# A graph layer on one Trainium2 core: each group's sums leave as 124 rows instead of 128

## The chip, the core and the metric

The program runs on one core of one Trainium2 chip. The metric is the device time of one execution in microseconds, and lower is better. Three executions of the kernel before took 2150.35, 2143.92 and 2141.62 us; the median is 2143.92 us.

## The reference, cut to what matters

There are 6250 nodes of 256 features and 100000 edges. Each edge has a source, a destination and two attributes, and the edges come **sorted by destination**. A graph attention layer comes first, then an expert layer; both add to `x`.

```python
h_fwd = h @ W_forward.T                      # h = layernorm(x); 64 outputs
h_rev = h @ W_reverse.T
messages = h_fwd[src] * direction[:, 0:1] + h_rev[src] * direction[:, 1:2]
scores = leaky_relu(einsum('ef,hf->eh', messages, attn), 0.2)     # 4 heads
exp_scores = exp(scores - scores.max(axis=0))
sum_exp = segment_sum(exp_scores, dst)       # per destination node and head
norm = exp_scores / (sum_exp[dst] + 1e-10)
outs = [segment_sum(messages * norm[:, hd:hd+1], dst) for hd in range(4)]
x = x + concat(outs)                         # 4 x 64 = 256 features
...
x = x + expert_layer(layernorm(x))           # 8 experts, the best one per token
```

So each node needs 260 sums over its incoming edges: 4 heads times 64 weighted message values, and 4 sums of exponentials. The change touches how these 260 sums per node reach memory.

## The kernel before

The kernel is one function, `tile_gnn_ffn_kernel`. A second function, `general_path`, computes the same for any input and runs at the end only if a flag says that the input broke an assumption of the first.

**Node table.** The first part (lines 667 to 698) normalises the nodes, multiplies them with the weights and stores `node_tab`, 136 floats (544 bytes) per node.

**Edge stage.** The edges are cut into 782 tiles of 128. Six tiles make a group (`GT = 6`, 131 groups), and two groups make a batch (66 batches). For each batch of 12 tiles, the loop from line 828 does this:

- GpSimd issues 12 indirect DMAs, one per tile (line 833), each gathering 128 rows of 544 bytes from `node_tab` into a slice of `gt`. `gt` has four buffers, so the gathers may run up to four batches ahead.
- VectorE scales and adds the two halves (lines 839 to 848), forms the scores (851 to 859), ScalarE takes the exponential (863), VectorE builds the weighted messages `v` (864, 865) and a matrix `hot` (870) that says which destination, counted from the group's first one, each edge has.
- For each of the two groups, TensorE adds up six products of `hot` and `v` into one PSUM tile `pv` (line 876): row k of it holds the 260 sums of the k-th destination after the group's first. One more small product (line 885) adds what the group before had gathered for the destination that both share.
- ScalarE copies `pv` to `r` in SBUF (line 887, four buffers), and SyncE loads the group's first destination from `base_i` into a register (888) and stores `r` at that row of `sums` (890).

The groups' stores **overlap**. A store always writes 128 rows from the group's first destination on, though the group reaches only as far as the next group's first destination; the store of the next group writes the rest over. So each store has to wait until the one before has landed, and the order of the stores is the order of the groups. Rows that a later store writes over don't matter.

The instruction order on each engine is the program's, reordered by a scheduler when the program is built. ScalarE's queue holds the exponentials and the copies of line 887 in one order, and a copy that waits holds up the exponential behind it. SyncE's queue in this stage holds the register load and the store of each group in turn, and nothing else.

**The check on the input.** `high` (line 759) is, for each group, how many rows further the next group begins. Line 785 sets a flag if any `high` is over 127, since rows between two stores would then be written by none.

**After the edge stage.** ScalarE's queue loads `sums` back in seven pieces `part` (line 951); VectorE divides, adds to `x` and normalises; the tokens are routed (line 1021), the experts run on TensorE (1046 to 1086), and the results are gathered and stored (1091 to 1107).

Of the kernel before, what the change touches and what calls it, by code (L numbers as in the profile page):

```python
# [11 lines left out]
OP = mybir.AluOpType  # L12
AX = mybir.AxisListType

P = 128
# [504 lines left out]
def kernel(  # L520
# [25 lines left out]
    nc = tc.nc  # L546
# [21 lines left out]
    NG = -(-ET // GT)  # L568
    EB = -(-ET // P)
    CHAIN = 16  # L570
    SPREAD = 40.0
    TROWS = N + P - 1
    NSLOT = E * CAP
# [5 lines left out]
    sums = dram.tile([TROWS, ACC], F32, name="sums")  # L579
# [183 lines left out]
    last_tile = local[:, GT - 1:GF * GT:GT]  # L763
    nc.vector.tensor_tensor(carry_from[:, CHAIN:GF], last_tile[:, CHAIN:GF], high[:, CHAIN:GF], OP.is_equal)

# [7 lines left out]
    wrong = ep.tile([P, 5], F32, name="wrong")  # L773
# [8 lines left out]
    nc.vector.tensor_reduce(wrong[:, 1:2], t0, AX.X, OP.max)  # L782
    nc.vector.tensor_scalar(wrong[:, 1:2], wrong[:, 1:2], 0.0, None, op0=OP.is_gt)
    nc.vector.tensor_reduce(wrong[:, 2:3], high, AX.X, OP.max)
    nc.vector.tensor_scalar(wrong[:, 2:3], wrong[:, 2:3], float(P - 1), None, op0=OP.is_gt)
    nc.vector.tensor_reduce(wrong[:, 3:4], high, AX.X, OP.min)
    nc.vector.tensor_scalar(wrong[:, 3:4], wrong[:, 3:4], 0.0, None, op0=OP.is_lt)
    nc.vector.memset(wrong[:, 4:5], 1.0)
    nc.vector.tensor_sub(t0[0:1, CHAIN:GF], high[0:1, CHAIN:GF], last_tile[0:1, CHAIN:GF])
    nc.vector.tensor_reduce(wrong[0:1, 4:5], t0[0:1, CHAIN:GF], AX.X, OP.min)  # L790
    nc.vector.tensor_scalar(wrong[:, 4:5], wrong[:, 4:5], 0.0, None, op0=OP.is_le)
# [19 lines left out]
    with tc.tile_pool(name="p2", bufs=3) as p2, \  # L811
# [8 lines left out]
        def over_partitions(to, t):  # L820

            pm = ps2.tile([P, H, P], F32, name="pm", tag="pv")
            for hd in range(H):
                nc.tensor.transpose(pm[:, hd, :], t[:, hd:hd + 1].to_broadcast([P, P]), ident)
            nc.vector.tensor_reduce(to, pm, AX.X, OP.max)

        before = None
        for b, gs in enumerate(batches):
            i0, i1 = gs[0] * GT, min((gs[-1] + 1) * GT, ET)
            n = i1 - i0  # L830
            gt = p2.tile([P, GB, ROW], F32, name="gt", bufs=4)
            for i in range(i0, i1):
                nc.gpsimd.indirect_dma_start(  # L833
                    out=gt[:, i - i0, :], out_offset=None, in_=node_tab,
                    in_offset=bass.IndirectOffsetOnAxis(ap=srci[:, i:i + 1], axis=0))
            m = p2.tile([P, GB, MS], F32, name="m")

            fac = turns[:, b % 2, 0:2, :]
            nc.vector.tensor_copy(fac[:, :, :n], ea[:, :, i0:i1])
            fw = gt[:, :n, 0:MS]  # L840
            nc.vector.tensor_mul(fw, fw, fac[:, 0, :n].unsqueeze(2).to_broadcast([P, n, MS]))  # L841
            for g in gs:
                a0, a1 = g * GT - i0, min((g + 1) * GT, ET) - i0
                k = a1 - a0
                rv = ps2.tile([P, GT, MS], F32, name="rv", bufs=1)
                nc.vector.tensor_mul(rv[:, :k, :], gt[:, a0:a1, MS:ROW],  # L846
                                     fac[:, 1, a0:a1].unsqueeze(2).to_broadcast([P, k, MS]))
                nc.vector.tensor_add(m[:, a0:a1, :], fw[:, a0:a1, :], rv[:, :k, :])  # L848
            sc = p2.tile([P, GB, H], F32, name="sc")
            s = sc[:, :n, :]  # L850
            nc.vector.scalar_tensor_tensor(s, m[:, :n, O:MS], 0.2, m[:, :n, O:MS],  # L851
                                           op0=OP.mult, op1=OP.max)
            if i1 == ET:
                nc.vector.tensor_scalar(sc[:, n - 1, :], sc[:, n - 1, :], no_edge, None, op0=OP.add)
            nc.vector.tensor_reduce(gmax[:, b, :], s.rearrange("p j h -> p h j"), AX.X, OP.max)
            if b == 0:
                over_partitions(shift, gmax[:, 0, :])
                nc.vector.tensor_copy(shift_p, shift)
            nc.vector.tensor_sub(s, s, shift_p.unsqueeze(1).to_broadcast([P, n, H]))
            v = p2.tile([P, GB, ACC], F32, name="v")  # L860
            w = fixed[:, P + H + (b % 2 * (2 + H) + 2) * GB:P + H + (b % 2 + 1) * (2 + H) * GB]
            w = w.rearrange("p (j h) -> p j h", h=H)
            nc.scalar.activation(v[:, :n, H * O:ACC], s, AF.Exp)  # L863
            nc.vector.tensor_copy(w[:, :n, :], v[:, :n, H * O:ACC])  # L864
            nc.vector.tensor_mul(  # L865
                v[:, :n, 0:H * O].rearrange("p n (h o) -> p n h o", h=H),
                m[:, :n, 0:O].unsqueeze(2).to_broadcast([P, n, H, O]),
                w[:, :n, :].unsqueeze(3).to_broadcast([P, n, H, O]))
            hot = p2.tile([P, GB, P], F32, name="hot")
            nc.vector.tensor_tensor(hot[:, :n, :], lane_p.unsqueeze(1).to_broadcast([P, n, P]),  # L870
                                    local[:, i0:i1].unsqueeze(2).to_broadcast([P, n, P]), OP.is_equal)
            for g in gs:
                tiles = list(range(g * GT, min((g + 1) * GT, ET)))
                pv = ps2.tile([P, ACC], F32, name="pv")
                for i in tiles:
                    nc.tensor.matmul(pv, hot[:, i - i0, :], v[:, i - i0, :], start=(i == tiles[0]),  # L876
                                     stop=(i == tiles[-1] and before is None))
                if before is not None:
                    k = (g - 1) % ZN
                    z = zt[(g - 1) // ZN % 2]  # L880
                    if k == 0:
                        nz = min(ZN, NG - g)

                        nc.vector.tensor_copy(z[:, 0:nz, 0], carry_from[:, g - 1:g - 1 + nz])
                    nc.tensor.matmul(pv, z[:, k, :], before, start=False, stop=True)  # L885
                r = p2.tile([P, ACC], F32, name="r", bufs=4)
                nc.scalar.copy(r, pv)  # L887
                row = nc.values_load(base_i[0:1, g:g + 1], engines=(mybir.EngineType.SP,), min_val=0,
                                     max_val=N - 1, skip_runtime_bounds_check_because="clamped to 0..N-1")
                nc.sync.dma_start(sums[bass.ds(row, P), :], r)  # L890
                before = r if g < CHAIN else v[:, tiles[-1] - i0, :]


# [5 lines left out]
        tiny = const.tile([P, H], F32, name="tiny")  # L899
        nc.vector.tensor_scalar(tiny, over, SPREAD, None, op0=OP.min)  # L900
        nc.scalar.activation(tiny, tiny, AF.Exp)
# [3 lines left out]

        nc.vector.tensor_scalar(bad[:, 0:1], bad[:, 0:1], SPREAD, 0.0, op0=OP.is_le, op1=OP.is_equal)
        nc.vector.tensor_reduce(bad[:, 1:2], wrong, AX.X, OP.max)
# [36 lines left out]
    with tc.tile_pool(name="p4", bufs=2) as p4, \  # L944
            tc.tile_pool(name="ps4", bufs=2, space=bass.MemoryType.PSUM) as ps4:
        for c in range(NCK):
# [48 lines left out]
            for n in range(CH):  # L995
# [12 lines left out]
                                           op0=OP.is_le, op1=OP.mult)  # L1008
# [7 lines left out]
                                    op0=OP.max, op1=OP.min)  # L1016
# [15 lines left out]
    with tc.tile_pool(name="p5", bufs=2) as p5, \  # L1032
# [13 lines left out]
        for e in range(E):  # L1046
# [26 lines left out]
            for a, b in rows:  # L1073
                k = b - a
                py = ps5.tile([P, D], F32, name="py")
                for f in range(FC):
# [8 lines left out]
                                               op0=OP.min, op1=OP.add)  # L1085
# [57 lines left out]
```

## Time and profile before

| what | value |
|---|---|
| median of three runs | 2143.92 us (2141.62 to 2150.35) |
| the profiled execution | 2147.85 us, of it 2146.1 us from the first to the last instruction |
| TensorE clock granted, mean | 0.735 of full speed |
| TensorE matmuls busy | 1146.4 us (53%) |
| VectorE busy | 917.6 us (43%) |
| GpSimd busy | 863.3 us (40%) |
| ScalarE busy | 224.8 us (10%) |
| edge stage, first gather to last store | about 100 to 1412 us |
| experts on TensorE | about 1580 to 2043 us |

All of the profile is of one execution, the one that took 2147.85 us. Busy shares are averages over very different stages, so the stages are read one by one. A row of the timeline gives the start, the duration, the engine, the line, the operation with the tile that it writes and those that it reads, and, in brackets, how long the engine was idle before and what ended that. In the rows, PE is TensorE, PEld its weight load, DVE VectorE, ACT ScalarE, POOL GpSimd, and SPq the queue of SyncE. "issue" means that the profile shows nothing that the engine waited for. A row of a table of stretches gives, for each engine, busy time and, in brackets, the number of instructions.

### The profile page before, as it was taken

To read this page: it belongs to the slowest core of one execution; us is meant where nothing else is said; L and a number is where in the kernel's file an instruction comes from. 1 tells how busy PE (TensorE), PEld (TensorE's weight loads), DVE (VectorE), ACT (ScalarE), POOL (GpSimd) and SP (SyncE) were. 2 spreads that over 40 slices of the span, in tenths; PEclk is the share of its full clock that TensorE was granted. 3 is DMA by queue.
4 is the path that set the end of the run, shared out by engine and by line. 5 is a ranking of instruction groups with operands and counts; after the bars stand their busy time and mean duration, and the time that the engine had idled before them with its cause. 6 is when DMAs were issued, how large, how long until landed. Compare 5 with 4: busy or idle time off the path is not lost. (4 is left out here: it accounts for less than half of the span.)

```text
span 2146.1 us, 13763 instructions
## 1 busy us (share of the span) xinstructions
PE 1146.4 (53%) x4158; PEld 840.2 (39%) x4158; DVE 917.6 (43%) x1827; ACT 224.8 (10%) x506; POOL 863.3 (40%) x896
## 2 busy tenths in 40 slices
PE   6421446434443454444334444545559999999900
PEld 5310334323232333333223333435436666666600
DVE  7540555544444455644345355657612222221134
ACT  2100000000000000000000000012211111111122
POOL 0176655555555665655556665103410000000065
PEclk9755677766666667766666766765569999999955
DMA  8522222222222222222222222162222222211034
GB/s 262 190 58 52 57 55 55 59 54 53 52 57 58 57 57 54 67 59 53 53 56 57 62 58 55 33 202 74 74 82 77 77 77 77 72 57 43 17 107 138
DMA packets 114150, 158.65 MB, mean 74 GB/s; under 512 B 19762, under 2 KB 94289, under 8 KB 113939
## 3 DMA queue, kind: packets, MB, share of 16 engines
q0 software_dynamic: 29728, 67.35, 13.8%
q1 hardware_dynamic: 66734, 74.20, 10.5%
q10 hardware_dynamic: 17604, 16.13, 2.4%
q8 instruction: 35, 0.57, 0.1%
q14 instruction: 49, 0.39, 0.1%
HBM read 107.80 MB, written 49.80 MB: 73 GB/s over the span
## 5 line engine op out<-in xcount | busy, mean ns | idle before, releaser
L833 POOL DMA_INDIRECT gt<-node_tab,srci x782 | 740.0, 946 | 623.0 <-DVE sc L851 278.7
L876 PE MATMUL pv<-v,hot 128*128 128x260 f32 x1564 | 498.1, 477 | 544.9 <-DVE hot L870 381.2
L876 PEld LDWEIGHTS pv<-v,hot 128*128 128x128 f32 x1564 | 370.3, 241 | 656.2 <-issue 578.5
L864 DVE COPY fixed<-v 128x48 f32<-128x48 f32 x66 | 13.9, 210 | 600.8 <-ACT v L863 393.7
L1097 POOL DMA_INDIRECT yg<-ybuf,to_get x49 | 64.9, 1325 | 484.4 <-issue 477.2
L1077 PE MATMUL py<-w2t,hf 128*128 128x256 f32 (+1 forms) x1024 | 222.3, 379 | 0.0
L865 DVE TENSOR_TENSOR v<-m,fixed 128x3072 f32<-128x3072 f32 x66 | 218.6, 3312 | 4.2
L1068 PE MATMUL ph<-xT,w1t 128*128 128x489 f32 (+1 forms) x512 | 213.9, 576 | 1.1 <-ACT hf L1070 1.0
L1077 PEld LDWEIGHTS py<-w2t,hf 128*128 128x128 f32 (+1 forms) x1024 | 189.6, 185 | 34.2 <-issue 3.5
L1080 DVE TENSOR_TENSOR y<-py,b2b 128x256 f32<-128x256 f32 x64 | 27.1, 424 | 359.1 <-PE py L1077 359.1
L887 ACT COPY r<-pv 128x260 f32<-128x260 f32 x131 | 48.4, 376 | 1053.2 <-issue 481.5
L1068 PEld LDWEIGHTS ph<-xT,w1t 128*128 128x128 f32 x512 | 95.8, 190 | 112.4 <-issue 104.2
L1070 ACT ACTIVATE hf<-ph,b1t 128x489 f32<-128x489 f32 (+1 forms) x128 | 84.4, 670 | 366.9 <-DMA xe<-buf 203.4
L885 PE MATMUL pv<-v,zt 128*128 128x260 f32 x228 | 81.6, 428 | 67.6 <-issue 67.6
L870 DVE TENSOR_TENSOR hot<-fixed,local 128x1536 f32<-128x1536 f32 x66 | 114.1, 1730 | 0.0
L1021 POOL DMA_INDIRECT buf<-h,to_put x49 | 56.2, 1147 | 106.0 <-DVE to_put L1015 66.7
L885 PEld LDWEIGHTS pv<-v,zt 128*128 128x128 f32 x228 | 51.9, 228 | 87.1 <-issue 78.6
L659 PE MATMUL pt<-ident,h 128*128 128x128 f32 x196 | 47.1, 361 | 69.0 <-DVE h L652 29.2
L841 DVE TENSOR_TENSOR gt<-gt,fixed 128x816 f32<-128x816 f32 x66 | 65.5, 993 | 29.0 <-DMA gt<-node_tab,srci 17.4
L848 DVE TENSOR_TENSOR m<-gt,rv 128x408 f32<-128x408 f32 x131 | 75.5, 576 | 4.5
L846 DVE TENSOR_TENSOR rv<-gt,fixed 128x408 f32<-128x408 f32 x131 | 76.1, 581 | 2.2
L885 PE MATMUL pv<-r,zt 128*128 128x260 f32 x32 | 13.3, 506 | 110.4 <-issue 71.9
(171 smaller groups left out, 747.9 us busy)
## 6 DMA issues: line engine op xcount, KB each, us to landing
sums<-r SPq DMA_DIRECT2D x131, 130.0 KB
gt<-node_tab,srci POOLq DMA_INDIRECT x782
w1t<-in_L_ffn_w_dram SPq DMA_DIRECT2D x8, 1024.0 KB
w2t<-in_L_ffn_w_dram SPq DMA_DIRECT2D x8, 1024.0 KB
buf<-zeros SPq DMA_DIRECT2D x15, 512.0 KB
xe<-buf ACTq DMA_DIRECT2D x56, 128.0 KB
ybuf<-y SPq DMA_DIRECT2D x56, 128.0 KB
part<-sums ACTq DMA_DIRECT2D x7, 910.0 KB
```

What stands on the lines that cost most here:

```text
L833: nc.gpsimd.indirect_dma_start(out=gt[:, i - i0, :], out_offset=None, in_=node_tab, in_offset=bass.IndirectOffsetOnAxis(ap=srci[:, i:i + 1 ...
L841: nc.vector.tensor_mul(fw, fw, fac[:, 0, :n].unsqueeze(2).to_broadcast([P, n, MS]))
L846: nc.vector.tensor_mul(rv[:, :k, :], gt[:, a0:a1, MS:ROW], fac[:, 1, a0:a1].unsqueeze(2).to_broadcast([P, k, MS]))
L848: nc.vector.tensor_add(m[:, a0:a1, :], fw[:, a0:a1, :], rv[:, :k, :])
L865: nc.vector.tensor_mul(v[:, :n, 0:H * O].rearrange("p n (h o) -> p n h o", h=H), m[:, :n, 0:O].unsqueeze(2).to_broadcast([P, n, H, O]), w[ ...
L870: nc.vector.tensor_tensor(hot[:, :n, :], lane_p.unsqueeze(1).to_broadcast([P, n, P]), local[:, i0:i1].unsqueeze(2).to_broadcast([P, n, P]) ...
L876: nc.tensor.matmul(pv, hot[:, i - i0, :], v[:, i - i0, :], start=(i == tiles[0]), stop=(i == tiles[-1] and before is None))
L885: nc.tensor.matmul(pv, z[:, k, :], before, start=False, stop=True)
L1068: nc.tensor.matmul(ph[:, :b - a], w1t[:, d, f * P:(f + 1) * P], xT[:, d, a:b], start=(d == 0), stop=(d == DC - 1))
L1070: nc.scalar.activation(hf[:, a:b], ph[:, :b - a], AF.Relu, bias=b1t[:, e * FC + f:e * FC + f + 1])
L1077: nc.tensor.matmul(py[:k, :], hid[f][:, a:b], w2t[:, f, :], start=(f == 0), stop=(f == FC - 1))
L1097: nc.gpsimd.indirect_dma_start(out=yg, out_offset=None, in_=ybuf, in_offset=bass.IndirectOffsetOnAxis(ap=to_get[:, j:j + 1], axis=0))
```

## The change

Each group but the last stores the first 124 rows of `r` instead of all 128. The last group still stores 128. The flag for the input is now set if a group's successor begins more than 124 rows further, since 124 rows from the group's first on are written.

```diff
@@ -568,6 +568,7 @@
     CHAIN = 16
+    WROWS = 124
     SPREAD = 40.0
@@ -782,7 +783,7 @@
     nc.vector.tensor_reduce(wrong[:, 2:3], high, AX.X, OP.max)
-    nc.vector.tensor_scalar(wrong[:, 2:3], wrong[:, 2:3], float(P - 1), None, op0=OP.is_gt)
+    nc.vector.tensor_scalar(wrong[:, 2:3], wrong[:, 2:3], float(WROWS), None, op0=OP.is_gt)
@@ -887,7 +888,8 @@
                 row = nc.values_load(base_i[0:1, g:g + 1], engines=(mybir.EngineType.SP,), min_val=0,
                                      max_val=N - 1, skip_runtime_bounds_check_because="clamped to 0..N-1")
-                nc.sync.dma_start(sums[bass.ds(row, P), :], r)
+                nr = P if g == NG - 1 else WROWS
+                nc.sync.dma_start(sums[bass.ds(row, nr), :], r[:nr, :])
```

The order of the instructions on every engine is the same in both kernels. Only the shape of 130 of the 131 stores on SyncE's queue differs, and one constant of one VectorE instruction.

## The prediction

> **What bounds the kernel now.** I read the page's list of costliest groups first, to see which engine waits in the edge stage.
>
> ```profile
> L833 POOL DMA_INDIRECT gt<-node_tab,srci x782 | 740.0, 946 | 623.0 <-DVE sc L851 278.7
> L887 ACT COPY r<-pv 128x260 f32<-128x260 f32 x131 | 48.4, 376 | 1053.2 <-issue 481.5
> ```
>
> GpSimd waits 278.7 us for VectorE to free a gather buffer, and ScalarE sits idle for 1053.2 us ahead of 131 short copies. Then two stretches of the stage.
>
> ```profile
> 522.00:822.00 300.00, 134.46 (x425) 101.61 (x424) 140.31 (x184) 13.39 (x45) 169.99 (x180) 0.68 0.24 55
> 1363.00:1412.00 49.00, 37.30 (x143) 29.97 (x141) 38.21 (x59) 5.22 (x16) 1.88 (x2) 0.89 0.10 31
> ```
>
> Columns: length, then PE, PEld, DVE, ACT, POOL. With gathers running, 300 us serve 180 gathers, 15 batches: 20.0 us a batch, and no engine is busy for more than 170 us. Once the gathers are over, the last ten stores' work (five batches) takes 49 us: 9.8 us a batch. So the gathers' presence costs, not the arithmetic. The timeline shows how.
>
> ```profile
> 701.74 0.95 POOL L833 DMA_INDIRECT gt<-node_tab,srci  x1 [15.90 <-DVE sc L851]
> ...
> 715.47 0.60 PE L885 MATMUL pv<-v,zt 128*128 128x260 f32 x2
> ...
> 728.41 0.38 PE L876 MATMUL pv<-v,hot 128*128 128x260 f32 x1 [0.28 <-issue]
> 729.81 0.19 PEld L876 LDWEIGHTS pv<-v,hot 128*128 128x128 f32 x1 [1.87 <-issue]
> 731.22 0.38 PE L876 MATMUL pv<-v,hot 128*128 128x260 f32 x1 [2.43 <-issue]
> ...
> 745.97 0.38 ACT L887 COPY r<-pv 128x260 f32<-128x260 f32 x1 [31.68 <-issue]
> 746.24 0.25 ACT L863 ACTIVATE v<-sc 128x48 f32<-128x48 f32 x1
> ```
>
> A burst of gathers starts at 701.74 and the next ones at 761.47 and 822.46, so the cycle is 60.4 us. In it go 36 gathers (three batches) at 1.25 us each, 45 us, and GpSimd then waits 15 to 16 us. TensorE ends a group at 716.1, yet ScalarE's copy of it runs at 745.97. Its `r` buffer can't be the reason: the copy four before it, at 692.28, was stored at once. In between, TensorE starts only one load or matmul every 1.40 us (728.41, 729.81, 731.22), instead of one every 0.2 us. When the burst is over at 746.4, all moves again. The exponential of 746.24 stood behind the copy, VectorE behind that, and the buffers of the gathers behind VectorE. So the stage is set by a convoy: while GpSimd gathers, TensorE's results come out late by some 30 us, once a cycle.
>
> What do the stores have in it? The DMA view of two short windows:
>
> ```profile
> DMA packets 288, 0.27 MB, mean 44 GB/s; under 512 B 32, under 2 KB 288, under 8 KB 288
> DMA packets 90, 0.08 MB, mean 23 GB/s; under 512 B 9, under 2 KB 90, under 8 KB 90
> ```
>
> The first, 692 to 698 us, holds two stores of `sums`: 256 rows and 32 small packets, 16 each. The second, 1986.4 to 1990 us, holds one store of 81 rows (`ybuf`): 81 rows and 9 small packets. The small ones have 4 bytes and come last on each DMA engine that took part: the completions that add to a semaphore. 128 rows use 16 engines and 81 use 9, both the largest divisor up to 16.
>
> ```profile
> SPq L890 <- DMA sums<-r: 89.5, 68, 3.0
> ```
>
> SyncE's stores do wait for each other, 89.5 us in 68 waits, as they must; but nobody listed waits long for them.
>
> **The change part by part.** *Rows.* 130 stores lose 4 rows of 1040 bytes: 0.54 MB of 158.65 MB. Worth nothing by itself: the DMA engines are busy for 24% of the stage.
>
> *Engines.* The largest divisor of 124 up to 16 is 4. So a store goes to 4 engines with 31 rows each instead of 16 with 8. The packet records of `sums` take 0.046 us a row, so 31 take 1.43 us and 8 take 0.37: a store is longer by 1.06 us (now 0.5 us of packets, about 2 us from issue to the next store's issue). The bounds from rows alone: no longer at all, if 16 engines are used after all, and 6.3 us in all, which the 127 rows stored at line 797 took one after another. I take 1.43, since both shapes shown follow the divisor.
> The Trainium skill, "DMA: Bandwidth & Descriptors", section on why a DMA increments its semaphore by 16, gives this very rule, and its rules for authors say to use all 16 engines, which speaks against the change. By that advice alone each store would cost about a microsecond more and the sum would be a loss of up to 130 times 1.06, 138 us; the rows say where it is hidden.
> What hides it: the next store comes 3 us or more later, or, after a release, queues for a while with four `r` buffers in hand (copies at 703.10, 706.16, 713.77 need stores that began 10 us before). Without this cover it would be 138 us. It is bare once, at the end: the second last store begins at 1409.9, the last waits for it until 1412.3, and the loads of `part` wait for the last. That is +1.0 us.
>
> *Completions.* A store posts 16 now and 4 then, a gather 16 in both. Per cycle that is 36 x 16 + 6 x 16 = 672 against 576 + 24 = 600, 10.7% less. Is this what TensorE's results queue behind? The trace hints at a crowd: of 14080 completions that the 880 indirect DMAs posted it recorded 3094, of 5290 of all others 4395. It doesn't show that TensorE waits for it. The bounds: nothing (the gathers alone fill it), and all of GpSimd's 278.7 us of waiting, when TensorE never falls behind. In between, if the 31.7 us wait goes with the completions: 10.7% of it is 3.4 us a cycle; if only the three stores between burst start and wait count (703.5, 706.6, 714.2), 36 of 624, 5.8%, 1.8 us. There are 698 gathers after the first 84, so 19.4 cycles: 66 us or 35 us. I take the middle, 51 us. A wait that shortens moves the next batch forward, and GpSimd's pause with it, until that pause (15 us a cycle) is used up.
> The same section of the skill says that the issuing queue itself writes the increments of the engines left out, at once; should these twelve count as one write, 5 replace 16 and the 51 us would be 47. No run shows it yet.
>
> *The constant* on line 785: nothing, one instruction of the same shape. It is also where the change could fail: the largest step between groups' first destinations is 97 in these inputs, so the flag stays off.
>
> **Sum.** 2147.85 + 1.0 - 51 = 2098 for the profiled execution. It ran 3.9 us above the median, so 2094 us for the median.
>
> **The rivals.** *Hidden, no change (0.30).* If TensorE is held by the gathers alone, only the +1.0 us is left: 2145 us, between 2134 and 2154. For it: 576 of 672 completions stay, and no row names the store as what anyone waits for.
>
> *Slower (0.25).* On four engines, 31 store rows stand in front of a gather's rows, so a gather lands up to 1.06 us later. VectorE's line 841 waits for gathers 13 times now; 13 x 1.06 is 14 us. If all 66 batches met it, 70 us. The middle, 42, gives 2186 us. It decides from where a batch's gathers land less than a microsecond ahead of their use. Against it: the burst from 701.74 fills buffers that VectorE uses from 757 us on.
>
> *The flag fires (0.01).* Then `general_path` runs as well, and the time at least doubles.
>
> **How the numbers follow.** Fewer completions have 0.44: the convoy is what costs, and it is sensitive, since a group 3 us earlier (ended at 713.0) got through with a wait of under a microsecond where the next one waited 30. That case spans 2045 (twice the middle) to 2133. About 0.5%, 11 us, is what a measurement can tell from no change: so faster 0.43, same 0.31, slower 0.26. The range from 2045 to 2190 leaves out the deeper gains, the worst of the late gathers and the flag.
>
> **What would show it.** Right: a window with two stores has 248 rows and 8 small packets; their packets take about 1.4 us; the cycle between bursts falls from 60.4 to about 58 us and GpSimd's 278.7 us of waiting to about 230; the stretch without gathers stays at 9.8 us a batch. The step on completions is wrong if the store posts 4 and the cycle stays. The step on cover is wrong if copies of line 887 wait for stores, or line 841 for gathers. The whole is wrong if 16 small packets per store remain.

## The result, and the profile after

| kernel | median | runs from to | ratio to before, 95% interval |
|---|---|---|---|
| before | 2144.73 us | 2134.74 to 2156.28 (20) | |
| 124 rows | 2140.82 us | 2134.70 to 2160.78 (20) | 0.999 [0.997, 1.001] |

The change makes no difference that can be measured. The forecast gain of 51 us is not there; the rival "hidden, no change" is what happened. The profiled execution of the changed kernel took 2150.88 us, 2149.2 us of it from the first to the last instruction, at a granted TensorE clock of 0.731. In its edge stage all line numbers are one higher (gather 834, exponential 864, `hot` 871, products 877 and 886, copy 888), and the store is line 892.

The change did do what it says. The DMA view of a window with two stores, 687.5 to 694.5 us, with its list of issues (KB of a store):

```profile
DMA packets 257, 0.27 MB, mean 39 GB/s; under 512 B 8, under 2 KB 256, under 8 KB 256
sums<-r SPq DMA_DIRECT2D x1, 125.9 KB
```

The window holds 8 small packets where there were 32, so each store uses 4 engines and posts 4 completions (256 less 8 are 248 rows, twice 124; the 257th packet is an instruction fetch). Over the whole execution the page counts 18201 packets under 512 bytes instead of 19762: 1561 fewer, and 130 stores with 12 fewer each are 1560. From the first to the last packet's end a store took 1.76 us (median) instead of 0.53, 1.23 us more where the prediction had 1.06.

Nothing followed from it in the stage. The page's groups of the changed kernel ("remote" means that a semaphore moved at the end of the wait and the profile finds no instruction beside it that moved it):

```profile
L834 POOL DMA_INDIRECT gt<-node_tab,srci x782 | 739.3, 945 | 623.3 <-DVE sc L852 294.5
L888 ACT COPY r<-pv 128x260 f32<-128x260 f32 x131 | 48.2, 375 | 1050.9 <-remote 488.1
```

The same two stretches as before (length, then PE, PEld, DVE, ACT, POOL; granted clock, DMA share, GB/s):

```profile
522.00:822.00 300.00, 134.93 (x435) 101.97 (x433) 144.16 (x187) 14.37 (x48) 173.20 (x184) 0.68 0.24 56
1363.00:1412.00 49.00, 36.93 (x142) 29.59 (x141) 38.20 (x59) 5.41 (x17) 1.89 (x2) 0.89 0.11 30
```

And its timeline from the start of a burst on:

```profile
695.70 0.94 POOL L834 DMA_INDIRECT gt<-node_tab,srci  x1 [15.93 <-DVE sc L852]
...
723.12 0.38 PE L877 MATMUL pv<-v,hot 128*128 128x260 f32 x1 [1.60 <-issue]
725.92 0.59 PE L877 MATMUL pv<-v,hot 128*128 128x260 f32 x1 [2.42 <-issue]
728.72 0.59 PE L886 MATMUL pv<-v,zt 128*128 128x260 f32 x1 [2.21 <-issue]
...
740.67 0.38 ACT L888 COPY r<-pv 128x260 f32<-128x260 f32 x1 [32.42 <-issue]
740.95 0.25 ACT L864 ACTIVATE v<-sc 128x48 f32<-128x48 f32 x1
```

GpSimd waits 294.5 us for VectorE where it waited 278.7; the prediction wanted about 230. ScalarE idles ahead of the copies as it did, 1050.9 us against 1053.2. The bursts still have 36 gathers and start at 695.70, 755.5 and 816.4, so the cycle is still 60 us, with a pause of 15.9 us ahead of it. Averaged from the second burst to the last two gathers, 36 gathers take 58.9 us in both profiles. The convoy is the same picture shifted by 6 us: matmul records 2.80 us apart with a weight load between (one TensorE instruction every 1.40 us), and a copy that ScalarE runs after 32 us, when the burst is over, with the exponential right behind it. The stretch without gathers is as before: 49 us with the same instructions in it.

The stores do wait longer for each other, 125.8 us instead of 89.5, but no copy of `pv` waits for one:

```profile
SPq L892 <- DMA sums<-r: 125.8, 66, 2.5
```

The one price that can be seen is at the end. SyncE's queue in the timeline, the last three stores, of the kernel before:

```profile
1406.60 6.01 SPq L890 DMA_DIRECT2D sums<-r  x3
```

The same three of the changed kernel:

```profile
1406.23 7.31 SPq L892 DMA_DIRECT2D sums<-r  x3
```

The three issues span 7.31 us instead of 6.01. Here no later group's work hides that a store waits for the one before: +1.3 us, where +1.0 was predicted. In the time of the whole, whose runs spread over 20 us, that can't be seen.

### The profile page after: what moved, and what is told of

The parts are those of the page before. It is cut to its first block, busy times and chain, and to the rows that moved or that the text cites. A ratio compares the mean times of both kernels' runs of the same rounds, so it can differ in the third digit from the quotient of the medians.

```text
span 2149.2 us, 13763 instructions
## 1 busy us (share of the span) xinstructions
PE 1155.7 (54%) x4158; PEld 844.8 (39%) x4158; DVE 917.6 (43%) x1827; ACT 224.3 (10%) x506; POOL 862.5 (40%) x896
## 2 busy tenths in 40 slices
DMA packets 112069, 158.10 MB, mean 74 GB/s; under 512 B 18201, under 2 KB 92208, under 8 KB 111858
## 5 line engine op out<-in xcount | busy, mean ns | idle before, releaser
L834 POOL DMA_INDIRECT gt<-node_tab,srci x782 | 739.3, 945 | 623.3 <-DVE sc L852 294.5
L877 PE MATMUL pv<-v,hot 128*128 128x260 f32 x1564 | 506.2, 481 | 534.1 <-DVE hot L871 373.5
L877 PEld LDWEIGHTS pv<-v,hot 128*128 128x128 f32 x1564 | 375.8, 245 | 652.9 <-issue 550.5
L866 DVE TENSOR_TENSOR v<-m,fixed 128x3072 f32<-128x3072 f32 x66 | 218.6, 3312 | 4.2
L1082 DVE TENSOR_TENSOR y<-py,b2b 128x256 f32<-128x256 f32 x64 | 27.1, 424 | 359.6 <-PE py L1079 359.6
L888 ACT COPY r<-pv 128x260 f32<-128x260 f32 x131 | 48.2, 375 | 1050.9 <-remote 488.1
L842 DVE TENSOR_TENSOR gt<-gt,fixed 128x816 f32<-128x816 f32 x66 | 65.6, 993 | 29.1 <-DMA gt<-node_tab,srci 17.7
```

The source lines that it names most:

```text
L834: nc.gpsimd.indirect_dma_start(out=gt[:, i - i0, :], out_offset=None, in_=node_tab, in_offset=bass.IndirectOffsetOnAxis(ap=srci[:, i:i + 1 ...
L866: nc.vector.tensor_mul(v[:, :n, 0:H * O].rearrange("p n (h o) -> p n h o", h=H), m[:, :n, 0:O].unsqueeze(2).to_broadcast([P, n, H, O]), w[ ...
```

## The experiments

The theory on trial is the prediction's: TensorE's results queue behind the completions that DMAs post, so fewer completions shorten the convoy (**completions**). Its rival: the gathers alone set the pace and the stores are covered (**gathers alone**). The other question is how far the cover of the stores reaches.

The comparisons of one set share a chip and its runs of the kernel before. That kernel took 2154.36 us (median) in the first set, 2153.75 us in the third, but 1827.69 us in the second, which ran on another chip; each number below is read against its own set.

### First set

**One engine for each store.** 113 is prime, so one engine takes all 113 rows and posts one completion.

```diff
-                nc.sync.dma_start(sums[bass.ds(row, P), :], r)
+                nr = P if g == NG - 1 else 113
+                nc.sync.dma_start(sums[bass.ds(row, nr), :], r[:nr, :])
```

> Each group but the last stores 113 rows, a prime number, and the check on the input is set to 113. By the divisor, a store should run on one DMA engine: 113 rows one after another, about 113 x 0.05 = 5.7 us of packets, and one completion instead of 16. If completions hold TensorE (the theory of the prediction, which the change already failed to bear out), removing 15 of 16 should shorten the 60 us cycle by about 14% of the 31.7 us wait, 4 us a cycle, 85 us in all. If the gathers alone hold TensorE and the store is hidden, the cycle between bursts stays at about 60 us; the cover should then break only where stores follow each other faster than about 7.5 us: in the ten groups at the end (4.9 us a group before), some 15 to 30 us, so about 2160 us. If every store's length were exposed, 130 x 5.2 = 680 us more.

Measured: 2192.55 us, 1.018 [1.013, 1.023], some 38 us slower, more than the 15 to 30 us expected. A store takes 6.02 us. SyncE's waits over the whole execution (microseconds in all, times, longest):

```profile
SPq L891 <- DMA sums<-r: 396.1, 64, 6.8
```

The waits of the copies between 1372 and 1462 us:

```profile
ACT r L887 <- DMA sums<-r: 37.5, 6, 7.3
```

The page's line of the gathers:

```profile
L833 POOL DMA_INDIRECT gt<-node_tab,srci x782 | 741.2, 948 | 630.7 <-DVE sc L851 286.1
```

SyncE waits 396.1 us for stores instead of 89.5, but GpSimd's wait, 286.1 us, neither falls nor grows, and the bursts of 36 mostly keep coming every 60 to 61 us (59.3 us on average, 58.9 in before). So 15 of 16 completions gone bring nothing, and stores eleven times as long cost nothing *while the gathers run*. The loss comes after the last gather: it starts at 1373.5 us, and from there to the issue of the last store are 84 us, where before has 48. Without the gathers a group takes 4.9 us (9.8 us a batch); stores that follow each other only every 7.4 us can't keep up with that, the `r` buffers run out, and ScalarE's copies wait for stores: the 37.5 us are all that they wait for stores in this execution.

**More completions.** Four stores of 16 rows of 4 bytes are added behind each group's store, to a scratch tensor that nobody reads: 64 more completions a group.

```diff
+    junk = dram.tile([64 * NG, 1], F32, name="junk")
...
+                for q in range(4):
+                    nc.sync.dma_start(junk[64 * g + 16 * q:64 * g + 16 * (q + 1), :], r[0:16, 0:1])
```

> After each group's store, SyncE issues four more tiny stores of 16 rows of 4 bytes from r to a scratch tensor, 16 DMA engines and 16 completions each. Completions per cycle rise from 672 to 672 + 6 x 64 = 1056, by 57%, with almost no bytes. If completions hold TensorE, the 31.7 us wait should grow by up to 57%, 18 us a cycle, 350 us in all; if only those ahead of the wait count, about half of that. If the gathers alone hold it, the time stays within 1% of 2144 us (SyncE's queue is longer by four issues of some 0.3 us and their lane waits a group, but a group has 10 us).

Measured: 2184.68 us, 1.016 [1.011, 1.021]. That is neither the 175 to 350 us of the theory nor within 1%, and a slowdown speaks for the theory; but the trace puts most of it elsewhere. The page's line of the gathers:

```profile
L834 POOL DMA_INDIRECT gt<-node_tab,srci x782 | 739.4, 945 | 627.4 <-DVE sc L852 291.2
```

The waits of the copies between 1353 and 1436 us:

```profile
ACT r L888 <- DMA junk<-r: 29.1, 6, 5.7
```

GpSimd waits as long as in the changed kernel (294.5), though a cycle now posts 6 x 64 = 384 completions more than the 672 of before (+57%). The last gather starts at 1368.4 us, 4 us later than in the profile of before. Most of the loss is in the copies' waits after it: there they wait for the scratch stores, and this tail is 65 us instead of 48. Of the 28 us between the two profiled executions that is 17; 7 more lie behind the last store. The run is not a clean one, since the added stores lengthen SyncE's queue as well: between 100 and 1353 us, too, copies wait for them, which they never did before.

```profile
ACT r L888 <- DMA junk<-r: 97.5, 16, 15.2
```

Even so the gathers keep their pace (36 of them in 59.3 us on average). A total alone would have spoken for the wrong theory here.

**Half of the products.** Three of a group's six products are left out, and with them half of each sum. The stores, gathers and completions stay.

```diff
-                for i in tiles:
+                half = tiles[::2]
+                for i in half:
```

> Only three of the six products of each group are summed (line 876), so TensorE's instructions in the edge stage fall from 7 to 4 a group; gathers, stores and all else stay. If TensorE's instructions pass at a fixed slow pace while GpSimd gathers (one load or matmul every 1.15 to 1.4 us), the wait falls with their number: 16 records instead of 28 a group, 18 us instead of 32, and the cycle of 60 us shrinks towards the 45 us that the gathers need: 200 to 280 us less, 1860 to 1940 us. If TensorE's results simply come out when the burst is over, whatever their number, the cycle stays at about 60 us and the time within 1% or 2% of 2144 us.

Measured: 2112.33 us, 0.983 [0.978, 0.989], with four runs spread from 2097.99 to 2129.93 us. The direction is the expected one, the size is not: some 40 us instead of 200 to 280. What it shows is the pace. The timeline in its first long burst, two copies and the product between them:

```profile
188.81 0.38 ACT L888 COPY r<-pv 128x260 f32<-128x260 f32 x1 [21.88 <-remote]
...
189.23 1.24 PE L886 MATMUL pv<-r,zt 128*128 128x260 f32 x2 [13.92 <-issue]
...
211.21 0.38 ACT L888 COPY r<-pv 128x260 f32<-128x260 f32 x1 [22.02 <-issue]
```

In the first 16 groups the carried product (line 886 in this kernel too) reads the copy of the group before, and is the last product of its own group. It is recorded as over at 190.5, yet the copy of that group's sum runs at 211.21, 22.4 us after the copy before it. A group now has 16 TensorE instructions (a product is two weight loads and two matmuls, and there are four products with the carried one). If their results come out one after another, that is 22.4 / 16 = 1.40 us each. TensorE's semaphore, as far as the trace holds its records, fits that: it moves at 188.78, which ends the first of the two waits, and at 205.58, and the three products in between are 12 instructions, 1.40 us each. In before a group has 28, and in the same burst its copies are 37.1 us apart, 1.33 us each:

```profile
178.17 0.38 ACT L887 COPY r<-pv 128x260 f32<-128x260 f32 x1 [37.97 <-remote]
215.27 0.38 ACT L887 COPY r<-pv 128x260 f32<-128x260 f32 x1 [36.72 <-remote]
```

The delay follows the number of TensorE instructions. The pace is that of the results, not of TensorE's recorded starts, which run ahead of them (1.24 us for the four instructions of the product above). The gain is small because GpSimd fills the time: bursts grow from 36 to 48 gathers in places, and a 77.5 us cycle of 48 is still 19.4 us a batch, against 20.

**Two gather buffers.** Could the rhythm of three batches a burst be that of the four `gt` buffers?

```diff
-            gt = p2.tile([P, GB, ROW], F32, name="gt", bufs=4)
+            gt = p2.tile([P, GB, ROW], F32, name="gt", bufs=2)
```

> gt has two buffers instead of four, so a burst can't be longer than 24 gathers, 30 us, and usually 12. If the convoy comes from long bursts (TensorE keeps up for about 13 us of a burst and falls behind after), short bursts with pauses between let TensorE through: a batch would then take the 15 us of its gathers plus a pause, 16 to 19 us instead of 20, 60 to 250 us less, 1890 to 2080 us. If the four buffers are what covers the wait, two make it worse: a batch would take 15 us of gathers and 10 us of VectorE one after the other, 25 us, 330 us more.

Measured: 2155.50 us, 1.001 [0.999, 1.003]. Only the first burst is shorter (60 gathers instead of 84); after it the bursts are 36 gathers again, 60 us apart. The buffers set neither, and nothing of what I expected came.

### Second set, on the other chip

**Two engines for each store.** 122 rows, 61 on each engine; otherwise the edit is that of 113 rows.

> Each group but the last stores 122 rows; by the divisor that is two DMA engines with 61 rows each, about 61 x 0.05 = 3.1 us of packets and 4.7 us from one store's issue to the next. The theory that the store is covered while gathers run and only the last ten groups feel it puts the decision where a store takes as long as a group at the end, 4.9 us: so two engines should still be hidden, and the time stay within 0.5% of the kernel before (+2 to +8 us for the last stores), although one engine with 113 rows took +1.8%. If a store's length costs in proportion anywhere else, two engines would give about half of the one engine's loss, +18 us.

Measured: 1833.02 us, 1.0027 [1.0017, 1.0038], +5.3 us. A store takes 3.2 us. The stretch from 522 to 822 us:

```profile
522.00:822.00 300.00, 174.06 (x568) 137.83 (x567) 186.76 (x246) 16.72 (x60) 226.86 (x241) 0.74 0.28 73
```

The page's line of the gathers:

```profile
L833 POOL DMA_INDIRECT gt<-node_tab,srci x782 | 739.5, 946 | 334.8 <-issue 232.8
```

Here 300 us serve 241 gathers, not 180: GpSimd issues all 782 back to back, one every 1.25 us, and no longer waits for VectorE. The convoy is missing on this chip; the kernel before, which has it on the other, took 1827.69 us here. The 18 us that a price in proportion would add are not there. The stores' price is at the end again: from the last gather (1076.0 us) to the issue of the last store are 27.1 us, and 21.0 in the run with half of a gather's bytes, which has the old stores and whose gathers take as long (976.6 us from the first to the last in both).

**No gathers after the fourth batch.** 734 of 782 gathers are left out; the later batches work on old rows.

```diff
-            gt = p2.tile([P, GB, ROW], F32, name="gt", bufs=4)
-            for i in range(i0, i1):
+            gt = gts[b % 4]
+            for i in range(i0, i1) if b < 4 else ():
```

> Only the first four batches are gathered; the others use the same four buffers again, so 734 of 782 gathers are left out. If the gathers' presence is what holds TensorE, the waits of ScalarE's copies vanish after the first batches, a batch takes about 9.8 us as it does at the end of the stage now, 66 x 9.8 = 650 us instead of 1310 us, and the whole about 1500 us. If TensorE is held by something else in the stage (its own clock, the stores, the copies), a batch stays well above 12 us.

Measured: one run, 1553.4 us beside 1827.69. The stretch from 500 to 800 us:

```profile
500.00:800.00 300.00, 224.90 (x805) 179.33 (x803) 267.12 (x350) 28.06 (x87) 0.00 (x0) 0.85 0.08 26
```

VectorE is busy for 267 of 300 us. ScalarE's 87 instructions are three a batch (two copies, one exponential), so 29 batches pass, 10.3 us each. So the arithmetic with all its stores needs 10.3 us a batch, GpSimd's gathers 15, and on the other chip the convoy makes it 20. As there was no convoy to remove here, the run doesn't show that without gathers it would go.

**Half of a gather's bytes.** Each gathered row has 272 bytes instead of 544; the second half stays zero.

```diff
-                    out=gt[:, i - i0, :], out_offset=None, in_=node_tab,
+                    out=gt[:, i - i0, 0:MS], out_offset=None, in_=node_tab.rearrange("n (k c) -> (n k) c", k=2),
```

> Each gather takes rows of 272 bytes instead of 544 (the second half of each row is left out and stays zero); the number of gathers, of rows and of completions is unchanged. If the bytes or the DMA engines' time hold TensorE, its pace in a burst (one load or matmul per 1.4 us) should nearly double and the 60 us cycle shrink towards 45 us: 1850 to 1950 us. If the issuing of gathers on GpSimd or their number holds it, the pace and the cycle stay, and the time within 1% to 2% of 2144 us.

Measured: one run, 1829.81 us beside 1827.69. A gather costs GpSimd 1.25 us whatever its bytes. Without a convoy the run could say nothing about the convoy, so it was repeated in the third set.

**Products in bfloat16.** `v` and `hot` become bfloat16, and so does `zt` from the 17th group on. A group has then half as many TensorE instructions, 14, with nothing left out; the factors are rounded to bfloat16.

```diff
-            v = p2.tile([P, GB, ACC], F32, name="v")
+            v = p2.tile([P, GB, ACC], BF16, name="v")
...
-            hot = p2.tile([P, GB, P], F32, name="hot")
+            hot = p2.tile([P, GB, P], BF16, name="hot")
```

> hot and v are bfloat16 (the products of line 876 still add up in PSUM as float32; the values of v are rounded). A float32 product shows as two loads and two matmuls in the profile, a bfloat16 one should show as one of each, so a group has 14 records instead of 28 after the first sixteen groups, and fewer than the 16 of the run with half the products. If TensorE's results pass at a fixed slow pace per instruction while gathers run, the gain is at least that run's 35 us, and more where VectorE writes half the bytes: 2020 to 2100 us. If the burst's end alone releases them, the gain is only VectorE's, 0 to 30 us.

Measured: 1821.70 us, 0.997 [0.995, 0.998]. With GpSimd as the bound there was little to gain: the last gather starts at 1074.7 us, about when it does with 122 rows (1076.0), and most of the gain of 6 us lies in the stretch behind it, 17 us to the issue of the last store (21.0 in the run with half of a gather's bytes, which has the same stores).

### Third set, on a chip with the convoy

**The changed kernel once more**, beside the others.

> The changed kernel itself, measured again beside the kernel before on the same chip. In the second set of runs the kernel before took 1828 us, not 2150 us, and no convoy was there: GpSimd issued its 782 gathers without a pause. If the store is hidden whatever sets the stage, the change costs only what follows the last gather, +1 to +3 us (two engines cost +5 us there): a ratio of 1.000 to 1.002 in either case. If fewer completions help where the convoy is and nothing where it isn't, the ratio is below 0.995 when the kernel before takes about 2150 us and 1.000 when it takes about 1828 us.

Measured: 2156.13 us, 1.001 [0.999, 1.003]. Bursts of 36, a cycle of 60 us, GpSimd waits 300.5 us for VectorE. It confirms the first result.

**More completions once more.**

> Four more tiny stores per group again, 57% more completions. The first time this cost +1.6%, and the trace put it behind the last gather: 65 us from there to the last store instead of 48. If completions don't hold TensorE, the loss is again 10 to 40 us and sits behind the last gather, whether the kernel before takes 1828 or 2150 us; the time from the first to the last gather stays within 1% of that of the kernel before. If they do, that time grows by 5% or more.

Measured: 2194.08 us, 1.019 [1.016, 1.022]. GpSimd's wait is 300.4 us, equal to that of the changed kernel in the same set. The last gather starts at 1377.6 us against 1370.6, and the tail after it is 69 us against 46. So of the difference to the changed kernel, 36 us in these two profiled executions, 22 us lie between the last gather and the last store, 7 in the whole gather stage, half a percent for 1056 completions a cycle instead of the changed kernel's 600, and the rest behind the last store.

**Half of a gather's bytes once more.**

> Rows of 272 bytes gathered instead of 544 again (the second half of each row is left out). Where gathers are back to back it changed nothing (1830 us beside 1828 us): a gather costs GpSimd 1.25 us whatever its bytes. Beside a kernel before of 2150 us it tells whether bytes make the convoy: then the cycle shrinks and the time falls below 2050 us; if the number of gathers makes it, the time stays within 2% of 2150 us.

Measured: one run, 2142.69 us beside 2153.75. The stretch from 522 to 822 us:

```profile
522.00:822.00 300.00, 138.51 (x440) 103.09 (x438) 143.99 (x188) 14.19 (x48) 173.81 (x184) 0.69 0.15 35
```

The DMA share falls from 0.24 to 0.15 and the rate from 55 to 35 GB/s, yet the cycle is still 58.9 us on average. It isn't the gathers' bytes that hold TensorE.

**Products in bfloat16 once more.**

> Products in bfloat16 again. Beside a kernel before of 1828 us, where the gathers are back to back, the gain was 6 us, all after the last gather. If TensorE's instructions pass at a slow pace while gathers run and that makes the convoy, the same kernel gains more beside a kernel before of 2150 us: 40 to 250 us. If it is 1828 us again, 5 to 8 us.

Measured: 2075.64 us, 0.964 [0.962, 0.966], 78 us faster than the kernel before: the version that beats both kernels. Two rows of the timeline:

```profile
606.05 0.38 ACT L889 COPY r<-pv 128x260 f32<-128x260 f32 x1 [12.90 <-issue]
...
625.00 0.38 ACT L889 COPY r<-pv 128x260 f32<-128x260 f32 x1 [18.58 <-issue]
```

The stretch from 522 to 822 us:

```profile
522.00:822.00 300.00, 57.02 (x251) 34.63 (x249) 162.38 (x216) 15.81 (x51) 188.01 (x199) 0.57 0.24 61
```

Within a burst these results come out 19.0 us apart: 14 instructions at 1.35 us each (18.3 us and 1.30 in the next burst, copies at 661.46 and 679.71). Now 300 us serve 199 gathers instead of 180, the cycle is about 55 us, and GpSimd waits 226.9 us for VectorE. Of the 82 us between this profiled execution and the changed kernel's of the same set, 71 lie between the first and the last gather. VectorE's work is no shorter: its two longest instructions of a batch, `v` and `hot`, take 3314 and 1731 ns, in before 3312 and 1730. The stores are the old ones with 16 engines. This is what the change would have had to do to gain: take away TensorE instructions, not completions.

## Why the prediction was wrong, point by point

- **Engines: right.** 124 rows go to 4 engines, 31 rows each. The Trainium skill's rule in "DMA: Bandwidth & Descriptors", section on why a DMA increments its semaphore by 16, agrees with every shape here: 130 stores of 124, 122 and 113 rows have 1561, 1821 and 1951 small packets fewer than those of 128, which is 12, 14 and 15 a store, and the stores get longer in step, 0.53 us on 16 engines, 1.76 on 4, 3.2 on 2 and 6.02 on one. The page's advice to use all 16 engines decides nothing while gathers run, because only the next store on SyncE's queue waits for a store.
- **Cover: right, with its limits now known.** The cover is the pace of the gather stage, 10 us a group on a chip with the convoy, 7.5 without. Stores of 6.02 us fit into the one, stores of 3.2 us into the other. After the last gather a group takes 4.9 us, and there each shape pays: 1.3 us for 4 engines, 5.3 for 2 (on the other chip) and some 38 for 1.
- **Completions: the step that failed.** This term of the sum, 51 us of gain, measured nothing. The chain of waits up to it was right: the convoy, the late copy, the exponential behind it, the buffers. (One reading of rows was not: between 716 and 746 us TensorE's recorded starts are 1.40 us apart only from 728.41 to 736.11; from 719.8 to 728.1 they come at the usual 0.2 us. It is the results that are late all the time.) The fault was in the next step. That few completions were recorded was read as a hint of a crowd, and a share of the wait was given to the stores by counting, although no row showed TensorE waiting for a completion. The few are the trace's records of semaphores; its packet records hold all 14080 and all 5290. The runs put something else in its place: from some 10 to 12 us into a burst of gathers on, TensorE's instructions come through one every 1.30 to 1.40 us, and the results of two groups are apart by their number of instructions times that (28 by 37.1 us, 16 by 22.4, 14 by 18.3 and 19.0). The first groups of a burst still pass almost at once (copies at 703.10, 706.16 and 713.77 in a burst from 701.74). Taking 12 or 15 of a store's 16 completions away, adding 57% to all of them, or halving the gathers' bytes leaves the cycle where it was, 58.9 to 59.8 us on average. The gathers' own 576 completions a cycle were not taken away by any run on this chip.
- **The page on the issuing queue's own increments: the trace agrees.** The packets show no such writes, but the trace's records of semaphores do. With 122 rows each of 130 stores has three records: one 0.41 us after its issue, before its first packet (0.9 us), and two when the data has landed. A store of 124 rows has at most five, and where it has five the first comes 0.42 us after its issue; one of 128 has up to 16, none before 1.5 us. So the twelve show as one write, and 47 us would have been the figure to take; since completions cost nothing here, 47 and 51 us were equally wrong.
- **Slower by late gathers: did not happen.** VectorE's wait for gathers is unchanged, 17.7 us in the page's line of 842 against 17.4 in that of 841 before.
- **Rows, the constant, the flag:** each as predicted, nothing. The flag stayed off.
- **The chances.** "Hidden, no change" had 0.30 with the right argument: no row names the store as what anyone waits for. It deserved the larger share. That the measured 2140.82 us lies between 2045 and 2190 is no merit of the sum: the range was wide enough to hold the case of no change.

What stays open is why TensorE's instructions come through so slowly during the gathers. The runs say what it depends on (the number of TensorE instructions) and what it does not (completions of stores, bytes, `gt` buffers). That it goes with the gathers is read from the traces, where results come out slowly only within bursts; the run without gathers was on the chip that has no convoy. The granted clock is no explanation: 0.68 with gathers and 0.89 after them is a factor of 1.3, and the pace differs by more than seven. What couples the two engines inside the chip, and why one of the two chips is without it, no run tells. One rival was not tested: the recording itself. On the chip with the convoy every trace with all gathers holds 2555 to 3539 of the indirect DMAs' 14080 semaphore records, on the other 14073 to 14078. So lost records go with the convoy; whether what loses them also holds TensorE, or the convoy loses them, is not shown.

## What to carry to other kernels

A resource that a change uses less of is worth nothing until a row shows someone who waits for it; where the trace shows a crowd but no waiter, give the gain a small chance, and test it by taking nearly all of the resource away and by adding half as much again. Where a total seems to speak for a theory, look where in the span the time lies before believing it: the added completions cost 30 us and more, but most of it behind the last gather. A transfer on fewer engines is free as long as the pace of the stage around it is longer than the transfer, and the place to look for its price is the tail, where that pace changes.

## What the runs showed of the hardware that was not expected

- The same program with the same inputs took about 2150 us on one chip and 1828 us on another. Most of the difference lies in the edge stage: in the traces of the one 180 gathers go in 300 us, in those of the other 241, and from the first gather to the last are 1264 us (before) against 977 (122 rows).
- On the slower chip, once a burst of gathers, one every 1.25 us, has lasted some 10 to 12 us, TensorE's results come through at one instruction every 1.30 to 1.40 us, in float32 and in bfloat16 alike. Once the gathers are over, a group of 28 of them takes 4.9 us in all, under 0.18 us each.
- An indirect gather of 128 rows keeps GpSimd for 1.25 us whether its rows have 272 or 544 bytes.
- The scratch stores, 64 rows of 4 bytes a group and their completions, raised the DMA engines' busy share of the stage from 0.24 to 0.54 (0.48 in the repeat). Most of it is in the records of the gathers' own packets (48.9% of 16 engines between 522 and 822 us, 19.5% in before; the stores' queue has 4.6%), and the pace of the stage hardly moved all the same.
- A store of SyncE on fewer than 16 engines shows one semaphore record more than it has engines, 0.4 us after its issue and ahead of its data: 3 records on 2 engines, at most 5 on 4.
